# Softmax denominators of an attention block: two 128x64 products, or four 64x64 products summed afterwards

## The chip, the cores and the metric

The kernel runs on one core of one Trainium2 chip. The metric is device time in microseconds (us) of one execution. Before the change it is 3827.91 us, the median of three runs (3826.85, 3827.91, 3833.11).

The engines are named as the profile names them: PE is TensorE (its weight loads stand apart as PEld), DVE is VectorE, ACT is ScalarE, POOL is GpSimd, SP is SyncE, which here only starts transfers.

## The reference, cut to what matters

Four layers act one after the other on an image of 512 channels and 64x64 pixels, each with a group normalisation ahead of it and a residual around it. The change touches only layer 0, an attention with 8 heads of 64 channels over all 4096 pixels:

```python
def _L0_conv_ref(fmap, wq, wk, wv, wo):
    ...
    q = to_tokens(_conv1x1(fmap, wq, gain_in))
    k = to_tokens(_conv1x1(fmap, wk, gain_in))
    v = to_tokens(_conv1x1(fmap, wv, gain_in))
    AA = jnp.sum(q * q, axis=-1)
    qk = jnp.einsum('bid,bjd->bij', q, k)
    sim = -(AA[:, :, None] + AA[:, None, :] - 2.0 * qk) * scale
    attn = jax.nn.softmax(sim, axis=-1)
    out = jnp.einsum('bij,bjd->bid', attn, v)
    out = out.reshape(B, h, H, W, d).transpose(0, 1, 4, 2, 3).reshape(B, h * d, H, W)
    return _conv1x1(out, wo, gain_out)
```

The softmax needs, for every head and query, the sum of the exponentials over the 4096 keys. That sum, the denominator, is what the change computes differently. Layers 1 and 2 are gated convolutions and layer 3 is a linear attention; they follow unchanged.

## The kernel before, in words

Everything is fp32 and one product of the array leaves two records in the trace. The attention is in `_attention_pairs` and works on two heads (a pair) at a time: rows 0 to 63 of a 128-row tile are the first head, rows 64 to 127 the second. For each of the 4 pairs, `project` makes queries and keys (and, for pairs 0 and 2, the values of two pairs) with products on the whole 128x128 array. Then come 8 blocks of 512 queries. A block walks over 32 tiles of 128 keys, index `t`:

- `scores` (lines 737 to 758) makes the 128 keys x 512 queries of both heads with four products on 64x64 quarters of the array (line 745). They go into a tile `ps_s` of two PSUM banks, one bank for each head. Two exponentials on ACT (line 753), one for each head, turn it into `pt` in SBUF.
- `values` (lines 760 to 770) multiplies `pt` with the values, again by four products on 64x64 quarters (line 765). It runs two tiles behind (`AHEAD = 2`). Keys 0 to 63 accumulate in the PSUM bank `av[0]`, keys 64 to 127 in `av[1]`.
- DVE adds `pt` into `acc` (line 832), 31 additions for each block. `acc` then holds, for each of 128 key rows and each head and query, the sum over the 32 tiles.

After the last tile, ACT copies `av[0]` to SBUF as `avs` (line 837) and DVE adds `av[1]` (line 842). What remains is to sum `acc` over its 128 rows, to divide, and to check that the denominators are in a safe range. That is `close` (lines 772 to 785). It is not run at once: block `b` is closed inside block `b+1`, after the scores of `t = 3` and ahead of the values of `t = 1`. There are 28 such closes (blocks 1 to 7 of 4 pairs). Block 7 of pairs 0, 1 and 2 is closed inside the next pair's `project`, after its second product step (3 closes), and the last block between two output products at the end (1 close).

In the last pair, `output` multiplies finished blocks with the output weights, on the 128x128 array (line 792): block `b-1` after each of the blocks 1 to 6, the last two at the end.

What sets the order around the change:

- Buffers. `ps_s` has 3 tiles of two banks, taken in turn by the scores, by the `ps_d` of `close`, by the products of `project` and by `output` (through `ps_mm`, which hands out the first half of such a tile). The tile that `ps_d` takes must have been emptied by the exponentials of `t = 1`. It is next wanted by the scores of `t = 6`. `av` has two single banks. `pt` has 5 buffers. The pool `p3` has three rows of 512 under the tag `row`, for `avs`, `rd` and the `kept` tiles of `project`.
- Queues. Each engine runs its instructions in the order of its own queue. A scheduler at build time places instructions of the program text in these queues, so that DVE, for example, has an addition to `acc` between two instructions of `close`.
- `project` keeps partial sums of its products (a Strassen-like scheme of seven products, `_Seven.steps`, lines 463 to 505). Step p1 goes to a bank which ACT copies to `kept` (line 664), and step p2 may accumulate on that bank only after the copy. Line 684 is the DVE addition that ends such a sum and frees its `kept` row.

Of the kernel before, what the change touches and what calls it, by code (L numbers as in the profile page):

```python
# [10 lines left out]
FP = mybir.dt.float32  # L11
# [5 lines left out]
P = 128  # L17
# [4 lines left out]
BLK = 512  # L22
# [3 lines left out]
D = C // HEADS  # L26
# [502 lines left out]
def _attention_pairs(tc, a, X, QO, gmask, small, centered, stats, mv, okay):  # L529
# [12 lines left out]
    nc = tc.nc  # L542
# [6 lines left out]
    with tc.tile_pool(name="att1", bufs=1) as p1, tc.tile_pool(  # L549
        name="att2", bufs=2  # L550
    ) as p2, tc.tile_pool(name="att3", bufs=3) as p3, tc.tile_pool(name="pt", bufs=5) as ptp, tc.tile_pool(
        name="ps_s", bufs=3, space=PSUM
# [8 lines left out]
        ps_mm = _Halves()  # L561
# [22 lines left out]
        ones = p1.tile([P, D], FP, tag="ones", name="ones")  # L584
# [186 lines left out]

        def close(pair, b, av, acc):

            ps = ps_mm.tile([P, BLK], FP, tag="mm", name="ps_d")
            for h in range(2):
                nc.tensor.matmul(
                    ps[h * D : (h + 1) * D, :], ones, acc[:, ts(h, BLK)], start=True, stop=True
                )
            rd = p3.tile([P, BLK], FP, tag="row", name="rd")
            nc.vector.reciprocal(rd, ps)  # L780
            nc.vector.tensor_mul(QO[pair][:, ts(b, BLK)], av, rd)
            nc.vector.scalar_tensor_tensor(
                good, rd, 1.0 / SUM_HIGH, good, ALU.is_ge, ALU.mult
            )
            nc.vector.scalar_tensor_tensor(good, rd, 1.0 / SUM_LOW, good, ALU.is_le, ALU.mult)
# [17 lines left out]

        for pair in range(HEADS // 2):
            project(pair, pair and (lambda: close(*done)))
            if pair == HEADS // 2 - 1:

# [6 lines left out]
            for b in range(NB):  # L814
# [3 lines left out]
                acc = p2.tile([P, 2 * BLK], FP, tag="acc", name="acc")  # L818
                pts = {}
                for t in range(NT + AHEAD):  # L820
                    if t < NT:
                        pts[t] = scores(pair, b, t)
                    if t == AHEAD + 1 and done is not None:
                        close(*done)
                    if t >= AHEAD:
                        u = t - AHEAD
                        pt = pts.pop(u)
                        values(home(pair), av, u, pt)
                        if u == 0:
                            first = pt  # L830
                        else:
                            add = nc.vector.tensor_add(acc, acc if u > 1 else first, pt)  # L832
                            if (pair, b, u) == (HEADS // 2 - 1, *HINT_DVE):
                                past(mybir.EngineType.DVE, add)
# [11 lines left out]
            if pair == HEADS // 2 - 1:  # L846
                output(NB - 2, range(2))
                close(*done)
# [6 lines left out]
        ps = ps_mm.tile([P, BLK], FP, tag="mm", name="ps_ok")  # L855
# [1271 lines left out]
```

## Time and profile before

One execution was profiled. Its span from the first to the last instruction is 3828.3 us, beside the median of 3827.91 us without the profiler's own view.

| | busy us | share of the span |
|---|---|---|
| PE, matrix products | 3752.0 | 98% |
| PEld, weight loads | 1657.9 | 43% |
| DVE | 2688.1 | 70% |
| ACT | 2069.3 | 54% |
| POOL | 132.2 | 3% |

The granted clock of the array is 0.996 of full speed over the span. By stages, in us from the start of the span:

| from, to | what | PE busy | DVE busy | ACT busy |
|---|---|---|---|---|
| 0 to 137 | loading, normalisation, `project` of pair 0 | 105.09 | 75.41 | 41.28 |
| 137 to 587 | 8 blocks of pair 0 | 449.08 | 345.62 | 327.19 |
| 640 to 1088 | 8 blocks of pair 1 | 448.00 | 344.63 | 326.29 |
| 1190 to 1638 | 8 blocks of pair 2 | 448.00 | 344.93 | 325.72 |
| 1692 to 2252 | 8 blocks of pair 3 with the output products | 560.00 | 392.08 | 327.90 |
| 2252 to 3828.3 | layers 1 to 3 | 1532.87 | 1055.22 | 676.70 |

How to read the views. A group line names the line of the kernel, the engine, the operation, what is written and read, its shape and count, then busy us, mean ns of one, and idle time of the engine just before with what ended it. A line of the timeline has the start in us, the length in us, engine, line and operation, and in square brackets how long the engine had been idle and what released it. Up to 8 matrix instructions in a row are merged into one line with a count. Ends of matrix products are modelled, so starts are the firmer numbers.

### The profile page before, as it was taken

How to read it: one execution, taken by the hardware profiler on the slowest of the kernel's cores; microseconds unless marked ns; L12 is line 12 of the kernel's file. 1: busy time of each engine (PE TensorE's matmuls, PEld its weight loads, DVE VectorE, ACT ScalarE, POOL GpSimd, SP SyncE). 2: the span in 40 equal slices, each digit the busy share in tenths (PEclk: the TensorE clock that was granted, in tenths of full speed). 3: DMA queues.
4: the chain of work that ended last, by engine and by line, in shares of the span. 5: the costliest groups of instructions: out<-in, count | busy, mean ns of one | idle time of the engine just before them, and what ended most of it. 6: DMA issues, size and time to landing. Idle time of an engine off the chain costs nothing. (4 is left out here: it accounts for less than half of the span.)

```text
span 3828.3 us, 81625 instructions
## 1 busy us (share of the span) xinstructions
PE 3752.0 (98%) x35294; PEld 1657.9 (43%) x35294; DVE 2688.1 (70%) x3242; ACT 2069.3 (54%) x2998; POOL 132.2 (3%) x112
## 2 busy tenths in 40 slices
PE   6999999999999999999999999999999999999999
PEld 5633334333365333343333334554445544455543
DVE  6577787777765777876776757766677677665437
ACT  3577774777735777746665655663246632355210
POOL 0000000000000000000000000000000000122112
PEclk9999999999999999999999999999999999999999
DMA  2000000000000000000000015772057730564312
GB/s 100 9 1 1 1 1 9 1 1 1 1 1 9 1 1 1 1 9 1 1 1 1 1 49 168 198 201 81 13 157 194 199 102 27 151 178 103 97 56 91
DMA packets 178413, 212.91 MB, mean 56 GB/s; under 512 B 13032, under 2 KB 121832, under 8 KB 177920
## 3 DMA queue, kind: packets, MB, share of 16 engines
q1 hardware_dynamic: 151232, 148.46, 14.5%
q10 hardware_dynamic: 26784, 59.11, 4.2%
q8 instruction: 280, 4.59, 0.5%
q14 instruction: 85, 0.70, 0.1%
q0 software_dynamic: 32, 0.06, 0.0%
HBM read 147.81 MB, written 59.77 MB: 54 GB/s over the span
## 5 line engine op out<-in xcount | busy, mean ns | idle before, releaser
L753 ACT ACTIVATE pt<-ps_s,A 128x512 f32<-128x512 f32 x2048 | 1286.3, 687 | 534.8 <-PE ps_s L745 527.1
L832 DVE TENSOR_TENSOR acc<-acc,pt 128x1024 f32<-128x1024 f32 x960 | 1174.1, 1223 | 327.8 <-ACT pt L753 300.8
L745 PE MATMUL ps_s<-O,K 64*64 64x512 f32 x8192 | 1111.6, 589 | 0.0
L745 PEld LDWEIGHTS ps_s<-O,K 64*64 64x64 f32 x8192 | 334.3, 133 | 553.8 <-issue 307.1
L765 PE MATMUL av<-pt,O 64*64 64x512 f32 x4096 | 558.2, 590 | 0.9 <-ACT pt L753 0.9
L765 PE MATMUL av<-pt,V 64*64 64x512 f32 x4096 | 554.4, 590 | 0.0
L1006 ACT COPY S<-S 32x1295 f32<-32x1295 f32 (+1 forms) x272 | 341.4, 1256 | 217.4 <-DMA S<-F 105.6
L765 PEld LDWEIGHTS av<-pt,O 64*64 64x64 f32 x4096 | 171.5, 133 | 276.1 <-issue 254.9
L765 PEld LDWEIGHTS av<-pt,V 64*64 64x64 f32 x4096 | 168.3, 133 | 281.0 <-issue 270.3
L933 PE MATMUL ps<-diff,w_sum 128*128 128x512 f32 x516 | 242.0, 601 | 3.1 <-DVE w_sum L441 1.9
L933 PEld LDWEIGHTS ps_cv<-S,T 64*32 64x32 f32 x13824 | 194.1, 105 | 111.5 <-issue 73.0
L933 PE MATMUL ps_cv<-S,T 64*32 64x128 f32 x13824 | 233.6, 273 | 5.0 <-issue 2.4
L933 PE MATMUL ps<-h,w_out_L 128*128 128x512 f32 x512 | 229.6, 599 | 1.5 <-DVE X L1287 1.4
L454 DVE TENSOR_TENSOR diff<-X 128x512 f32<-128x512 f32 x200 | 134.0, 683 | 83.1 <-PE ps L933 46.4
L383 ACT ACTIVATE X<-X,gn_less 128x512 f32<-128x512 f32 x122 | 77.3, 709 | 152.0 <-DVE gn_less L125 152.0
L933 PE MATMUL ps<-X,w_in_L 128*128 128x512 f32 x304 | 145.8, 611 | 10.8 <-ACT w_in_L L391 5.4
L933 PE MATMUL ps<-h,pw_L 128*128 128x512 f32 x320 | 143.8, 599 | 1.9 <-DVE h L1275 1.6
L933 PEld LDWEIGHTS ps<-h,w_out_L 128*128 128x128 f32 x512 | 94.0, 190 | 118.3 <-issue 96.5
L933 PEld LDWEIGHTS ps<-diff,w_sum 128*128 128x128 f32 x516 | 94.6, 190 | 116.8 <-issue 106.5
L454 DVE TENSOR_TENSOR diff<-X,diff 128x512 f32<-128x512 f32 x200 | 135.3, 683 | 12.9 <-PE ps L933 11.3
L1060 DVE STREAM_TRANSPOSE h<-ps_cv 128x512 f32<-128x512 f32 x112 | 109.2, 1048 | 48.6 <-PE ps_cv L933 48.2
L933 PE MATMUL ps<-agg,w_proj 128*128 128x512 f32 x256 | 118.5, 602 | 1.0 <-DVE turned L1060 0.9
(233 smaller groups left out, 3324.7 us busy)
## 6 DMA issues: line engine op xcount, KB each, us to landing
T<-in_L_T_dram SPq DMA_DIRECT2D x112, 384.0 KB, 4.6
F<-plane ACTq DMA_DIRECT2D x112, 324.0 KB, 3.5
S<-F SPq DMA_DIRECT2D x224, 162.0 KB, 4.6
S<-G SPq DMA_DIRECT2D x96, 153.0 KB, 4.3
G<-plane ACTq DMA_DIRECT2D x48, 289.0 KB, 2.5
row<-G SPq DMA_DIRECT2D x48, 272.0 KB, 3.3
T<-in_L_T_dram SPq DMA_DIRECT2D x48, 256.0 KB, 4.1
out_dram<-y SPq DMA_DIRECT2D x32, 256.0 KB, 2.0
```

Of the source, the lines that this page charges most:

```text
L383: self.nc.scalar.activation(xs, xs, AF.Identity, bias=less)
L454: yield eng.tensor_tensor(t[j][c], a(c), b(c), ALU.subtract)
L745: nc.tensor.matmul(ps[ts(half, D), ts(h, BLK)], K[rows, t * P + half * D : t * P + (half + 1) * D], QO[pair][rows, cols], start=True, stop ...
L753: exp = nc.scalar.activation(pt[:, ts(h, BLK)], ps[:, ts(h, BLK)], AF.Exp, bias=A[:, t, h : h + 1])
L765: nc.tensor.matmul(av[half][rows, :], v[keys, t * P + h * D : t * P + (h + 1) * D], pt[keys, ts(h, BLK)], start=(t == 0), stop=(t == NT - 1),)
L832: add = nc.vector.tensor_add(acc, acc if u > 1 else first, pt)
L933: self.tc.keep_in_program_order(self.nc.tensor.matmul(*args, **kw))
L1006: nc.scalar.copy(second, first)
L1060: nc.vector.transpose(out, src)
```

## The change

Inside `close`, the ones that sum `acc` over its rows are used in two halves of 64 rows. Four products of 64x64 quarters take the place of two products of 128x64: rows 0 to 63 of `acc` go to the first bank of `ps_d`, rows 64 to 127 to the second, and within a bank the first head fills partitions 0 to 63 and the second 64 to 127. The two banks are then added: ACT copies the first to `rd`, DVE adds the second to it. The reciprocal that read PSUM before now reads and writes `rd` in SBUF. `ps_d` now has both banks of its `ps_s` tile in use, where the second stood empty before. Nothing else differs.

```diff
         def close(pair, b, av, acc):
 
-            ps = ps_mm.tile([P, BLK], FP, tag="mm", name="ps_d")
-            for h in range(2):
-                nc.tensor.matmul(
-                    ps[h * D : (h + 1) * D, :], ones, acc[:, ts(h, BLK)], start=True, stop=True
-                )
+            ps = ps_s.tile([P, 2 * BLK], FP, tag="s", name="ps_d")
+            for half in range(2):
+                keys = slice(half * D, (half + 1) * D)
+                for h in range(2):
+                    nc.tensor.matmul(
+                        ps[ts(h, D), ts(half, BLK)],
+                        ones[keys, :],
+                        acc[keys, ts(h, BLK)],
+                        start=True,
+                        stop=True,
+                    )
             rd = p3.tile([P, BLK], FP, tag="row", name="rd")
-            nc.vector.reciprocal(rd, ps)
+            nc.scalar.copy(rd, ps[:, 0:BLK])
+            nc.vector.tensor_add(rd, rd, ps[:, BLK:])
+            nc.vector.reciprocal(rd, rd)
             nc.vector.tensor_mul(QO[pair][:, ts(b, BLK)], av, rd)
             nc.vector.scalar_tensor_tensor(
                 good, rd, 1.0 / SUM_HIGH, good, ALU.is_ge, ALU.mult
```

## The prediction, made before the changed kernel had run

> **What bounds the kernel now.** I read the page's busy shares first, then busy time by stages, then the groups of `close`, and last the timelines of PE, ACT and DVE around one close (pair 0, block 2, about 254 us) and around the close inside the `project` of pair 2.
>
> ```profile
> PE 3752.0 (98%) x35294; PEld 1657.9 (43%) x35294; DVE 2688.1 (70%) x3242; ACT 2069.3 (54%) x2998; POOL 132.2 (3%) x112
> ```
>
> PE is busy for 98% of the span and in the blocks for all of it, so the array's sequence of starts sets the time there. ACT and DVE have room: about 326 and 345 of 448 us for a pair's eight blocks.
>
> A busy array can still lose time between products. The PE timeline shows where:
>
> ```profile
> 253.32 1.04 PE L745 MATMUL ps_s<-O,K 64*64 64x512 f32 x8
> 254.29 1.08 PE L776 MATMUL ps_d<-acc,ones 128*64 128x512 f32 x4
> 255.29 1.09 PE L765 MATMUL av<-pt,O 64*64 64x512 f32 x8
> 256.20 1.04 PE L745 MATMUL ps_s<-O,K 64*64 64x512 f32 x8
> 257.06 1.04 PE L765 MATMUL av<-pt,O 64*64 64x512 f32 x8
> ```
>
> Four quarters run side by side, in two passes, so scores or values of one tile take two intervals. Their length comes from weight loads far apart in a block:
>
> ```profile
> 2177.92 0.15 PEld L745 LDWEIGHTS ps_s<-O,K 64*64 64x64 f32 x4 [0.28 <-PE ps_s L745]
> 2219.12 0.15 PEld L745 LDWEIGHTS ps_s<-O,K 64*64 64x64 f32 x4 [0.28 <-PE ps_s L745]
> ```
>
> These are 24 key tiles, 96 intervals, apart: 41.20 / 96 = 0.4292 us. From the scores at 253.32 to the next at 256.20 there are six intervals (scores, `ps_d` and values, two each), or 2.575 us at that pace. It took 2.88: 0.305 us are lost around `ps_d`. From starts it splits into 0.11 ahead of `ps_d`, 0.14 ahead of the values and 0.05 after their first pass.
>
> Whole blocks say the same. The copies of `av` that end two blocks:
>
> ```profile
> 250.12 0.59 ACT L837 COPY avs<-av 128x512 f32<-128x512 f32 x1 [1.30 <-PE av L765]
> ...
> 306.23 0.59 ACT L837 COPY avs<-av 128x512 f32<-128x512 f32 x1 [1.30 <-PE av L765]
> ```
>
> A block with a close is 32 x 4 + 2 = 130 intervals, 55.79 us; it took 56.11, an excess of 0.32. Over the blocks of the first three pairs it is steadily 56.10 to 56.11. I use 0.312 for a close.
>
> **What the Trainium skill says.** "TensorEngine Tiling (Array Packing)", Tiling Modes, Key Properties: changing the tiling mode, not merely the tile, drains the engine. Scores and values use 64x64 and `ps_d` 128x64, so each close inside a block has two mode changes; the trace agrees, at 0.31 us for both. The same page, Gotcha 1 under Restrictions and Gotchas, says different row tiles cannot access one PSUM bank at the same time. This is why the four quarters need two banks and an addition; no trace tests it. "Perfetto Trace Analysis", Tensor Engine Instruction, says that ends of matrix instructions are estimated, so I count starts only; the 1.04 us lengths overlap the following starts here. "TensorE: Matmul & The Clock Gate", Architectural detail, says ACT and DVE are strict FIFO: a copy added to ACT's queue holds up the exponentials behind it if it waits.
>
> **The change part by part.** *Array.* `ps_d` becomes four quarters in two passes, two intervals of 0.4292 us, the form that line 765 already has (rows choose the bank, columns the partitions). Before, two products in two passes took two intervals too. Weight loads go from 4 to 8 records, as in every other 64x64 group, under running products. So the useful array time is unchanged and only the two mode changes go: 28 x 0.312 = 8.7 us. For the three closes in `project` and the last one the neighbours are 128x128: both mode changes stay, and I take 0 (at most the same 0.3 us each way).
>
> *Start of `ps_d`.* Without the drain it starts at 254.18. It still needs the tile that the second key tile's exponentials free. ACT runs the first four tiles' exponentials from 250.99 to 255.73, so that one is over at about 253.36, the load being wanted at about 253.75. That covers it, by 0.4 us.
>
> *ACT copy and DVE addition.* Nearest rows are the copy and addition of `avs`, of the same shapes, and the reciprocal:
>
> ```profile
> L780 DVE RECIPROCAL rd<-ps_d 128x512 f32<-128x512 f32 x32 | 107.2, 3349 | 0.0
> L842 DVE TENSOR_TENSOR avs<-avs,av 128x512 f32<-128x512 f32 x32 | 22.0, 687 | 19.3 <-ACT avs L837 18.4 <-ACT mark L840 0.9
> L837 ACT COPY avs<-av 128x512 f32<-128x512 f32 x32 | 18.8, 586 | 41.5 <-PE av L765 41.5
> ```
>
> That is 32 x 0.586 = 18.8 us more ACT and 32 x 0.687 = 22.0 us more DVE. The reciprocal from SBUF instead of PSUM is shown by no row; a tenth either way is 0.33 us for each, off the path, and I take no difference.
>
> In the queues of the changed build the copy stands behind the eight exponentials of the first four tiles, and the addition and reciprocal behind the third addition to `acc` (it was behind the second). Behind the copy waits the exponential of `t = 4`. ACT was idle there:
>
> ```profile
> 250.99 4.74 ACT L753 ACTIVATE pt<-ps_s,A 128x512 f32<-128x512 f32 x8 [0.28 <-PE ps_s L745]
> 257.31 1.26 ACT L753 ACTIVATE pt<-ps_s,A 128x512 f32<-128x512 f32 x2 [1.58 <-PE ps_s L745]
> ```
>
> The quarters are finished by about 255.3, the copy runs 255.73 to 256.32, and the scores of `t = 4`, 0.3 us earlier than now, release their exponential at about 257.0. It fits. On DVE:
>
> ```profile
> 254.78 1.23 DVE L832 TENSOR_TENSOR acc<-acc,pt 128x1024 f32<-128x1024 f32 x1
> 255.92 3.35 DVE L780 RECIPROCAL rd<-ps_d 128x512 f32<-128x512 f32 x1
> 259.19 1.16 DVE L832 TENSOR_TENSOR acc<-acc,pt 128x1024 f32<-128x1024 f32 x1
> ```
>
> The third addition takes 255.92 to 257.15, the new one ends at about 257.85 and frees `ps_d`'s tile. It is wanted by the scores of `t = 6`, whose loads would stand at about 258.9. So the release moves ahead of the need by 1 us. Today it is just late, and harmless:
>
> ```profile
> 259.32 0.15 PEld L745 LDWEIGHTS ps_s<-O,K 64*64 64x64 f32 x4 [0.39 <-DVE rd L780]
> 259.64 0.15 PEld L745 LDWEIGHTS ps_s<-O,K 64*64 64x64 f32 x4 [0.17 <-issue]
> ```
>
> The first load is 0.11 late, the second is back on the pace. This wait goes and gives nothing. The fourth addition to `acc` ends near 263.5. It gates the exponential of `t = 9` (five `pt` buffers), due near 265.6: cover 2 us.
>
> *`project`.* In pairs 1 and 3 the copy waits for a `kept` row freed by DVE at about 598.7, the addition frees the bank at about 600.6, and the addition of line 684 that p2's copy depends on moves ahead of the reciprocal: no delay. In pair 2 the order is worse:
>
> ```profile
> 1099.11 3.36 DVE L780 RECIPROCAL rd<-ps_d 128x512 f32<-128x512 f32 x1
> ...
> 1104.13 0.68 DVE L684 TENSOR_TENSOR V<-ps,kept 128x512 f32<-128x512 f32 x1
> ...
> 1103.70 0.59 ACT L664 COPY kept<-ps 128x512 f32<-128x512 f32 x1 [9.02 <-DVE O L781]
> ...
> 1104.33 0.33 PEld L458 LDWEIGHTS ps<-X,wqkv 128*128 128x128 f32 x2 [0.53 <-ACT kept L664]
> ```
>
> Today the copy starts when line 781 frees the row of `avs`, and PE's p2 starts on the pace at 1104.47. In the changed build it waits for the addition to `V` (line 684) behind the reciprocal. DVE now runs: addition to `O` until 1100.1, the new addition until 1100.75, reciprocal until 1104.1, `V` until 1104.7. So `kept` is ready at 1105.35 instead of 1104.29, and p2 starts 1.0 us late. PE is busy throughout this stage, so I count it in full: +1.0 us, once; between 0 and 2.
>
> *End.* The last quotient is finished at 2236.2 today, about 1.4 us later with the copy and addition. The output product that needs it starts after fourteen other passes, about 2240.6: hidden by 3 us.
>
> Sum: -8.7 + 1.0 = -7.7 us. The profiled span goes from 3828.3 to 3820.6. Its difference to the median is 0.4 us, so I subtract from the median: 3820.2 us.
>
> **Rivals.**
> A: no drain is saved, since the gap belongs to something else at this place (the trace credits the load of `ps_d` to an exponential). Against it: that exponential ended 0.8 us earlier, and the same long load gap stands at other changes of form. Saving 0, `project` +1: 3828.9 us.
> B: the released tile comes late. If the copy or addition gets behind one more key tile's work than I read in the queues, the tile comes free at 259.6 instead of 257.85, 0.7 us after its need. The stall repeats in 28 blocks: 28 x 0.7 = 19.6, less the saving of 8.7, plus 1: 3839.8 us. It decides from a release about 1.3 us later than mine, where the stall eats the 0.31. For it: two more links in the chain. Against it: these are the queue orders of the built program, and 1 us of slack.
> C: half of the saving stays hidden, because the wait of `ps_d` for its tile has only 0.4 us cover and a late exponential shifts it, or because `project` loses 2 to 4 us instead of 1: 28 x 0.15 = 4.2 less 1, or 8.7 less 4: about 3824 us.
>
> **How the numbers follow.** My forecast gets 0.78, A 0.06, B 0.08, C 0.08. The forecast's own range is 3818 to 3822: the excess could be 0.30 to 0.33 us, `project` 0 to 2, the four outer closes 1 us either way. About 0.2%, 7.7 us, is what a measurement of this kernel can tell from no change, and the forecast stands at that edge. One fact leans it towards the faster side: PE catches up with a late load in part (as at 259.64), and I counted the stall in `project` in full. I put 0.50 of its 0.78 beyond and 0.28 within. A and C lie within, which makes 0.42. B is slower: 0.08. The range is 3817.8 to 3826.5; it holds the forecast and C, and leaves out A and B.
>
> **What would show it.** In the PE timeline of the changed kernel, scores of `t = 3` to scores of `t = 4` take 2.58 us instead of 2.88, blocks take 55.79, `ps_d` stands as one line of 8 products 64x64, and the load that waited for `rd` waits for nothing on DVE. In `project` of pair 2 one load waits about 1 us for `kept`. I am wrong if blocks still take 56.1 (A), if the loads of line 745 wait for line 787 (the new addition) or those of `ps_d` for an exponential (B, C), or if the three `project` stages grow by more than 2 us together.

## The result, and the profile after

| | before | changed |
|---|---|---|
| median | 3831.12 us (10 runs) | 3822.26 us (10 runs) |
| span of the profiled execution | 3828.3 us | 3821.6 us (its time 3823.27 us) |
| block with a close inside, pairs 0 to 2 | 56.10 to 56.14 us, one 56.20 | 55.79 to 55.80 us |
| block of the last pair with output products | 70.19 to 70.20 us | 69.88 to 69.92 us |
| stage from pair 0 to 1, 1 to 2, 2 to 3 | 107.85, 157.86, 107.85 us | 107.89, 158.38, 107.89 us |
| first to last copy of `av` | 2029.23 us | 2020.91 us |
| from the last copy of `av` to the end | 1605.08 us | 1607.95 us |

The ratio of the times is 0.9978, with a 95% interval of 0.9969 to 0.9986: the changed kernel is faster by 8.9 us in the medians. Blocks and stages are counted from one copy of `av` to the next (line 837 before, line 845 after). The row "first to last copy of `av`" is the attention; it is 8.32 us shorter. The spans of the two profiled executions differ by less, 6.7 us: what lies ahead was 1.2 us shorter, but the layers behind the attention took 2.9 us more in that execution. The part on the scatter below comes back to this.

The busy shares of the page after:

```profile
PE 3741.6 (98%) x35422; PEld 1915.0 (50%) x35422; DVE 2717.5 (71%) x3274; ACT 2085.0 (55%) x3030; POOL 133.4 (3%) x112
```

128 more products and loads on PE (x35294 before), 32 more instructions each on DVE and ACT. PE stays the bound. Two copies of `av` that end two blocks, in the ACT timeline after:

```profile
248.53 0.59 ACT L845 COPY avs<-av 128x512 f32<-128x512 f32 x1 [1.27 <-PE av L765]
...
304.32 0.59 ACT L845 COPY avs<-av 128x512 f32<-128x512 f32 x1 [1.27 <-PE av L765]
```

They are 55.79 us apart, which is 130 intervals of 0.4292 us and nothing more. The PE timeline around `ps_d` of the same close (start, length, line, operation, count):

```profile
250.76 0.75 PE L765 MATMUL av<-pt,O 64*64 64x512 f32 x4
251.19 0.59 PE L745 MATMUL ps_s<-O,K 64*64 64x512 f32 x1
251.34 0.60 PE L765 MATMUL av<-pt,O 64*64 64x512 f32 x3
251.62 0.75 PE L745 MATMUL ps_s<-O,K 64*64 64x512 f32 x4
252.05 0.59 PE L778 MATMUL ps_d<-acc,ones 64*64 64x512 f32 x1
252.20 0.60 PE L745 MATMUL ps_s<-O,K 64*64 64x512 f32 x3
252.48 0.75 PE L778 MATMUL ps_d<-acc,ones 64*64 64x512 f32 x4
252.91 0.59 PE L765 MATMUL av<-pt,O 64*64 64x512 f32 x1
253.06 0.60 PE L778 MATMUL ps_d<-acc,ones 64*64 64x512 f32 x3
253.34 0.75 PE L765 MATMUL av<-pt,O 64*64 64x512 f32 x4
253.76 0.59 PE L745 MATMUL ps_s<-O,K 64*64 64x512 f32 x1
```

From the scores of `t = 3` (251.19) to those of `t = 4` (253.76) pass 2.57 us, where it was 2.88. The other thing to see is the counts of 1 and 3: one quarter of the array runs ahead of the other three. It starts `ps_d` at 252.05, the three follow at 252.63 (within the row at 252.48, one interval ahead of their second pass at 253.06): 0.58 us apart, and so in every row. The four quarters are four streams with a pace of 0.4292 us each. The distance arises in the first block of a pair, which has no close, in the kernel before as well; there the first `ps_d`, at the start of the second block, ends it. In the changed kernel it then stays as it is through all blocks of a pair, 0.58 us in pairs 0 and 2 and about 0.46 us in pair 1, until products in another form stand between, as the output products do in the last pair.

ACT and DVE at the same close, one timeline each:

```profile
249.43 4.74 ACT L753 ACTIVATE pt<-ps_s,A 128x512 f32<-128x512 f32 x8 [0.31 <-PE ps_s L745]
254.02 0.62 ACT L786 COPY rd<-ps_d 128x512 f32<-128x512 f32 x1
255.44 1.27 ACT L753 ACTIVATE pt<-ps_s,A 128x512 f32<-128x512 f32 x2 [0.80 <-PE ps_s L745]
```

```profile
253.22 2.56 DVE L840 TENSOR_TENSOR acc<-acc,pt 128x1024 f32<-128x1024 f32 x2
255.69 0.68 DVE L787 TENSOR_TENSOR rd<-rd,ps_d 128x512 f32<-128x512 f32 x1
256.41 3.35 DVE L788 RECIPROCAL rd<-rd 128x512 f32<-128x512 f32 x1
```

The copy follows the eight exponentials at once and is done 0.80 us before the next one can start. The addition frees the tile of `ps_d` at 256.37. The weight loads of the scores of `t = 6`, which take that tile, in the timeline of loads:

```profile
256.34 0.30 PEld L765 LDWEIGHTS av<-pt,O 64*64 64x64 f32 x4
256.77 0.13 PEld L745 LDWEIGHTS ps_s<-O,K 64*64 64x64 f32 x1
256.92 0.15 PEld L765 LDWEIGHTS av<-pt,O 64*64 64x64 f32 x3
257.20 0.30 PEld L745 LDWEIGHTS ps_s<-O,K 64*64 64x64 f32 x4
```

No load of line 745 waits for `rd` any more (before, line 780 held up such loads for 11.2 us in 28 waits). The first of the `ps_s` loads stands at 256.77, 0.40 us behind the release, that of the other three about 257.35.

### The profile page after: what moved, and what is told of

The parts are those of the page before. It is cut to its first block, busy times and chain, and to the rows that moved or that the text cites. A ratio compares the mean times of both kernels' runs of the same rounds, so it can differ in the third digit from the quotient of the medians.

```text
span 3821.6 us, 81915 instructions
## 1 busy us (share of the span) xinstructions
PE 3741.6 (98%) x35422; PEld 1915.0 (50%) x35422; DVE 2717.5 (71%) x3274; ACT 2085.0 (55%) x3030; POOL 133.4 (3%) x112
## 5 line engine op out<-in xcount | busy, mean ns | idle before, releaser
L745 PE MATMUL ps_s<-O,K 64*64 64x512 f32 x8192 | 1459.2, 589 | 0.0
L765 PE MATMUL av<-pt,O 64*64 64x512 f32 x4096 | 800.5, 589 | 0.9 <-ACT pt L753 0.9
L745 PEld LDWEIGHTS ps_s<-O,K 64*64 64x64 f32 x8192 | 483.3, 133 | 430.5 <-issue 234.8
L765 PE MATMUL av<-pt,V 64*64 64x512 f32 x4096 | 660.3, 589 | 0.0
L765 PEld LDWEIGHTS av<-pt,O 64*64 64x64 f32 x4096 | 284.2, 133 | 162.2 <-ACT pt L753 11.9
L765 PEld LDWEIGHTS av<-pt,V 64*64 64x64 f32 x4096 | 205.2, 133 | 269.0 <-issue 258.3
L941 PE MATMUL vkp<-kT,vT 128*128 128x512 f32 x256 | 115.4, 593 | 3.0 <-DVE vT L1700 2.0
```

Source lines behind the costliest of these rows:

```text
L745: nc.tensor.matmul(ps[ts(half, D), ts(h, BLK)], K[rows, t * P + half * D : t * P + (half + 1) * D], QO[pair][rows, cols], start=True, stop ...
L765: nc.tensor.matmul(av[half][rows, :], v[keys, t * P + h * D : t * P + (h + 1) * D], pt[keys, ts(h, BLK)], start=(t == 0), stop=(t == NT - 1),)
L941: self.tc.keep_in_program_order(self.nc.tensor.matmul(*args, **kw))
```

## Experiments

**Which of the two parts counts?** The form of the products and the chain behind them (copy, addition, reciprocal from SBUF) were tried apart. `form_alone` puts `ps_d` into quarters but only over rows 0 to 63, so half of each denominator is left out and one bank holds the result; the chain is that of before.

```
-  ps[h * D : (h + 1) * D, :], ones, acc[:, ts(h, BLK)], start=True, stop=True
+  ps[ts(h, D), :], ones[0:D, :], acc[0:D, ts(h, BLK)], start=True, stop=True
```

> Only the form of the products changes: two products in 64x64 quarters over rows 0 to 63 of acc, one bank, the reciprocal straight from PSUM as before. Rows 64 to 127 of acc are left out of the denominators. Theory (the drain is gone, but the tile of ps_d is now held too long: the reciprocal, which starts after the second addition to acc, frees it about 9.2 us after the block's av copy, and the scores of t = 6 now want it at about 8.3 to 8.9): blocks take 56.1 to 56.3, so nearly all of the gain is lost to the wait for rd, about 0.4 us in each block; the total is 3829 to 3833, no faster than before. Rival (as the prediction put it, that wait gives nothing and costs nothing): blocks take 55.79 and the total falls by 8 us.

`chain_alone` keeps the 128x64 products and takes the longer chain; the bank is added to its own copy, so the denominators are doubled.

```
-  nc.vector.reciprocal(rd, ps)
+  nc.scalar.copy(rd, ps)
+  nc.vector.tensor_add(rd, rd, ps)
+  nc.vector.reciprocal(rd, rd)
```

> Only the chain of ACT copy, DVE addition and reciprocal from SBUF; the products stay 128x64 and the DVE adds the same bank again, so denominators are doubled. Theory (two mode changes for each close stay): blocks take 56.10, the wait for rd is gone from the loads of line 745, the project of pair 2 is longer by 0.5 us; the total is that of before plus 0 to 1. Rival (the gain came from freeing the tile earlier, not from the form): blocks take 55.79.

`form_copy` is `form_alone` with an ACT copy that frees the bank and a reciprocal from SBUF; half of each denominator is left out here too.

> The quarters over rows 0 to 63 of acc with an ACT copy that frees the bank, and the reciprocal from SBUF; no second bank and no addition, so rows 64 to 127 are left out of the denominators. Theory (form and early release are needed together): blocks take 55.79, no load of line 745 waits for rd, total 8 to 9 us below before. Rival (two quarters behave otherwise than four, or the addition matters): blocks take more than 55.9.

| kernel | block | first to last copy of `av` | ratio to before (95%) |
|---|---|---|---|
| before, run again | 56.10 us | 2029.22 us | |
| `form_alone` | 55.84 us | 2022.10 us | 0.998 (0.9971 to 0.9989) |
| `chain_alone` | 56.10 us | 2029.60 us | 1.0002 (0.9993 to 1.0011) |
| `form_copy` | 55.79 us | 2021.80 us | 0.9978 (0.9972 to 0.9985) |

(The first close of each pair, up to 0.04 us longer in three of the four kernels, is left out of the second column, and so is one block of 56.19 us in each of the first two.) The form alone brings 0.26 of the 0.31 us of a block; the chain alone brings nothing, though it too takes away the wait of the loads for `rd`. My theory for `form_alone`, that this wait would eat most of what the form gains, fell. The loads of `form_alone` show why (in brackets the idle time before):

```profile
257.33 0.15 PEld L765 LDWEIGHTS av<-pt,O 64*64 64x64 f32 x2 [0.22 <-issue]
257.75 0.15 PEld L765 LDWEIGHTS av<-pt,O 64*64 64x64 f32 x2 [0.28 <-issue]
258.61 0.21 PEld L745 LDWEIGHTS ps_s<-O,K 64*64 64x64 f32 x8 [0.71 <-DVE rd L780]
```

The pairs of loads at 257.33 and 257.75 belong to the quarters that also did `ps_d`. Their next load was due at 258.18 and came at 258.61, 0.43 us late. But a load runs one pass, 0.43 us, ahead of its product, so the product was 0.05 us late, as the block is. (The two quarters that had no `ps_d` to do were two passes ahead and could wait.)

`form_copy` lost 0.76 us in each of the stages from pair 0 to 1 and 2 to 3 (108.61 us), where the order of PE's products around `ps_a` came out differently (that this costs the 0.76 us was not tested); the stage from pair 1 to 2 took 157.88.

**Does the loss belong to the change of form or to the place?** The denominators were summed a second time, in a block's quiet middle, in the form of each kernel (`twice_before`, `twice_after`). The copy at the end of `again` reads one element of the second sum, which is used for nothing else.

```
                         close(*done)
+                    if t == 11 and done is not None:
+                        again(done[3])
```

```
+        def again(acc):
+            ps = ps_mm.tile([P, BLK], FP, tag="mm", name="ps_e")
+            for h in range(2):
+                nc.tensor.matmul(
+                    ps[h * D : (h + 1) * D, :], ones, acc[:, ts(h, BLK)], start=True, stop=True
+                )
+            nc.scalar.copy(none, ps[0:1, 0:1])
```

In `twice_after` the four quarter products stand in `again`, in a tile of two banks from the pool of the scores.

> The kernel before, with a second set of the two denominator products in 128x64 tiles (tile `ps_e`, read only in one element) at key tile 11 of each block that has a close inside. Two more passes are 0.858 us. If the 0.31 us belong to the two changes of tiling mode, wherever they stand, these blocks go from 56.10 to 56.10 + 0.858 + 0.31 = 57.27 us. If they belong to the place behind the third scores (rival A: the wait of `ps_d` for its tile), they go to 56.10 + 0.858 = 56.96.

> The changed kernel, with a second set of the four quarter products (tile `ps_e`, read only in one element) at key tile 11 of each block that has a close inside. If no change of mode means no loss, blocks go from 55.79 to 55.79 + 0.858 = 56.65 us. If four more quarters bring a loss of their own at a place where nothing waits, 56.8 or more.

Measured, in one execution each: blocks of 57.27 us in `twice_before` and 56.65 us in `twice_after`, both to 0.01 us what the theory of the mode changes gives. The PE timeline of `twice_before` at the new place:

```profile
267.15 1.04 PE L765 MATMUL av<-pt,O 64*64 64x512 f32 x8
268.01 1.04 PE L745 MATMUL ps_s<-O,K 64*64 64x512 f32 x8
268.98 1.08 PE L791 MATMUL ps_e<-acc,ones 128*64 128x512 f32 x4
269.99 1.09 PE L765 MATMUL av<-pt,O 64*64 64x512 f32 x8
270.90 1.04 PE L745 MATMUL ps_s<-O,K 64*64 64x512 f32 x8
```

Groups are 0.86 us apart (267.15 to 268.01); into the 128x64 form it takes 0.97, out of it 1.01, and 0.91 behind: 0.11 + 0.15 + 0.05 = 0.31 us, the split seen at the first place. The 0.31 us are the price of going from 64x64 to 128x64 tiles and back. Rival A fell.

It is not that the 128x64 products themselves are slow. The second pass of `ps_e` starts 0.48 us after the first, and so does that of the 64x64 values behind it: 0.05 us over the pace in both. Each of the two changes costs about 0.16 us, 0.11 or 0.10 up to the first start and 0.05 up to the second. The loads show how. In the timeline of loads of `twice_before`:

```profile
268.01 0.15 PEld L745 LDWEIGHTS ps_s<-O,K 64*64 64x64 f32 x4 [0.28 <-issue]
268.98 0.20 PEld L791 LDWEIGHTS ps_e<-acc,ones 128*64 128x64 f32 x4 [0.81 <-ACT pt L753]
269.99 0.21 PEld L765 LDWEIGHTS av<-pt,O 64*64 64x64 f32 x8 [0.81 <-issue]
```

Within the stream a load stands a pass ahead of its product. At each change of form it starts together with its product instead (268.98 and 269.99 in both timelines), which agrees with a drain. In `twice_after` the first load of `ps_e` keeps its lead of 0.43 us:

```profile
267.32 0.13 PEld L801 LDWEIGHTS ps_e<-acc,ones 64*64 64x64 f32 x1
```

```profile
267.75 0.59 PE L801 MATMUL ps_e<-acc,ones 64*64 64x512 f32 x1
```

**How late may the tile come free?** One (`late1`) or three (`late3`) operations on `rd` that leave it as it is, ahead of the new addition:

```
+            for _ in range(3):
+                nc.vector.scalar_tensor_tensor(rd, rd, 1.0, rd, ALU.mult, ALU.max)
             nc.vector.tensor_add(rd, rd, ps[:, BLK:])
```

> The changed kernel with one more operation of 0.68 us on `rd` ahead of the new addition, which leaves `rd` as it was: the tile of `ps_d` comes free at 257.07 instead of 256.37. The loads of the scores of t = 6 stand at 256.77 (one quarter) and 257.35 (three) and run a pass ahead of their products, so nothing is lost: blocks of 55.79 to 55.85 us, the total within 2 us of the changed kernel. Rival: PE has no slack at the release, then each block gains up to 0.68 us and the total 19 us.

> As late1 with three such operations: the tile comes free at 258.4. The three quarters that load at 257.35 are 1.1 us late, of which the 0.43 us by which a load runs ahead of its product hides a part: blocks of 56.5 us (56.3 to 57.1), the total +20 us (+14 to +37) on the changed kernel, and the loads of line 745 wait for `rd`. If the place of the release doesn't matter at all, blocks of 55.79 us and no change.

In one execution each, `late1` has blocks of 55.79 us (span 3819.3 us), `late3` of 56.83 us, with three longer ones (span 3855.6 us, time 3857.3 us: slower than the kernel before, 3832.05 us in the same series). DVE and loads of `late1`:

```profile
256.69 0.69 DVE L789 TENSOR_TENSOR rd<-rd,ps_d 128x512 f32<-128x512 f32 x1
```

```profile
257.13 0.14 PEld L765 LDWEIGHTS av<-pt,O 64*64 64x64 f32 x3 [0.28 <-issue]
257.49 0.21 PEld L745 LDWEIGHTS ps_s<-O,K 64*64 64x64 f32 x5 [0.21 <-issue]
```

The release at 257.38 makes the first quarter's load, due at 257.12, 0.37 us late, and it costs nothing. DVE, loads and PE of `late3`:

```profile
258.96 0.69 DVE L789 TENSOR_TENSOR rd<-rd,ps_d 128x512 f32<-128x512 f32 x1
```

```profile
257.92 0.18 PEld L765 LDWEIGHTS av<-pt,O 64*64 64x64 f32 x4 [0.25 <-issue]
259.77 0.24 PEld L745 LDWEIGHTS ps_s<-O,K 64*64 64x64 f32 x8 [1.66 <-ACT pt L753]
```

```profile
257.92 1.07 PE L765 MATMUL av<-pt,O 64*64 64x512 f32 x8
259.80 1.09 PE L745 MATMUL ps_s<-O,K 64*64 64x512 f32 x8 [0.81 <-DVE rd L789]
```

The loads were due at 258.35 and came at 259.77, just behind the release at 259.65 (the view of loads names an exponential, long done; PE's names `rd`). 1.42 us late, less the pass by which they run ahead, makes 1.0, and the block is 1.04 us longer. I had taken the three operations at 0.68 us each; with the gaps they moved the addition by 2.22 us (258.96 against 255.69, each counted from its own copy of `av`, 249.58 and 248.53), and the stall came out above the 0.7 us of the expectation, within its range. `late1` moved it by 0.79 us for nothing. If each microsecond beyond the free ones costs one in a block, 2.22 - 1.04 = 1.2 us are free; this is an estimate, as no run lies between the two. `late3` is rival B made real.

**Is there a better mixture?** `hybrid` takes the new form only inside blocks and leaves the three closes in `project` and the last one as they were.

```
-                        close(*done)
+                        close(*done, inside=True)
```

(`close` picks the old or the new body by `inside`.)

> Quarters, copy and addition only in the closes that stand inside a block; the closes in `project` and the last one keep the form of before. Blocks of 55.79 us as in the changed kernel; the stage from pair 1 to pair 2 goes from 158.38 back to 157.86, if the +0.5 us there come from the longer chain (copy, addition, reciprocal) ahead of the addition to `V`. If they come from anything else in the changed kernel, they stay. The total is 0.5 us below the changed kernel, which the times can't tell from nothing: ratio to before 0.997 to 0.999.

> The changed kernel again. Blocks of 55.79 us and 2020.9 us from the first to the last copy of `av`, as before; the rest of the span (1608 us behind the last copy) moves by 2 or 3 us, if what it lost there against the kernel before is scatter between executions. The ratio to before 0.9970 to 0.9985.

The attention went as expected: blocks of 55.79 us, the stage from pair 1 to 2 at 157.90 us, 2020.41 us in all against 2020.90. But the median was 3825.83 us (ratio 0.9987, 0.9981 to 0.9994) beside 3823.31 us for the changed kernel in the same series (0.9979, 0.9971 to 0.9987). Both went again:

> The kernel of `hybrid` again, beside the changed kernel, since its median stood 2.5 us above that of the changed kernel while its attention was 0.5 us shorter. If that was scatter between executions, the two medians come within 1.5 us of each other, in either order, and the time behind the last copy of `av` goes with the granted clock. If the mixed form costs something behind the attention, it stands 2 to 3 us above again.

> The changed kernel for comparison: 2020.9 us from the first to the last copy of `av`, ratio to before 0.997 to 0.9985.

3827.84 us (0.9987, 0.998 to 0.9995) beside 3824.86 us (0.998, 0.9972 to 0.9989). The mixture stands 2.5 and 3.0 us above again, so by the expectation on record this isn't scatter alone, though the intervals overlap. Its attention is shorter in both traces, and behind the last close the order of instructions on PE, ACT, DVE, POOL and SP is the same in both kernels. What makes it longer there stays open. One part can be seen, in the busy times of a 200 us stretch in the layers behind the attention; the number before the DMA share is the granted clock. `hybrid` and `hybrid_2`:

```profile
2414.20:2614.20 200.00, 193.61 (x3566) 100.04 (x3565) 142.24 (x205) 121.51 (x107) 0.00 (x0) 0.98 0.64 177
```

```profile
2414.20:2614.20 200.00, 194.95 (x3667) 101.55 (x3666) 142.61 (x206) 123.19 (x107) 0.00 (x0) 1.00 0.64 177
```

The same program got a clock of 0.98 in one execution and 1.00 in the other; behind the last copy of `av` they took 1613.7 and 1609.7 us. Counted at the same products, these 4.0 us are lost inside this stretch, so the clock can account for the distance between the two executions of `hybrid` (0.02 of 200 us), but not for two medians above those of the changed kernel. No version was found that beats the changed kernel.

## The prediction, step by step

**Array: right.** 28 x 0.312 = 8.7 us was the saving. Added up, the 28 blocks are 8.92 us shorter. Most gained 0.31 us; I had overlooked that the first close of each pair stands in a block of 56.13 to 56.14 us before, where the quarters also come together again, and that one block took 56.20. That the loss goes with the changes of mode, of which the Trainium skill, "TensorEngine Tiling (Array Packing)", Tiling Modes, Key Properties, says that they drain the engine, is shown by the second set of products: another 0.31 us at another place in the 128x64 form, none in quarters.

**"This wait goes and gives nothing": right, nearly.** `chain_alone` removes it and gains nothing in a block; `form_alone` keeps it, 0.43 us late at its load, and loses 0.05 us.

**Start of `ps_d`, copy and addition: right.** Counted from its copy of `av`, this close stands 1.59 us earlier than before (248.53 against 250.12). The copy was put at 255.73, so here at 254.14, and ran at 254.02. Its cost was taken from the copy of `avs`, 586 ns; the rows of the tile `ps_d` after show (shortest, median and longest, ns):

```profile
L786 ACT COPY rd<-ps_d x32: 586/625/629, 198.2 to 2221.7; 128x512 f32<-128x512 f32 x32
L787 DVE TENSOR_TENSOR rd<-rd,ps_d x32: 677/681/689, 199.9 to 2222.4; 128x512 f32<-128x512 f32 x32
```

It is 625 ns in 28 of 32 cases, where it follows exponentials at once; the 0.04 us more lie in ACT's idle 0.80 us. The reciprocal from SBUF takes 3352 ns, from PSUM 3349: no difference, as I took it.

One sign that I had named for rival C is there, at no cost: a load of `ps_d` that comes just behind an exponential. The quarter that runs ahead has used up the cover of 0.4 us. In the timeline of loads after, its first load follows the end of the second tile's exponentials (about 251.86) and stands 0.14 us ahead of its product at 252.05, where 0.43 is usual; the product is still on the pace, 0.43 us after the one before (251.62).

```profile
251.91 0.44 PEld L778 LDWEIGHTS ps_d<-acc,ones 64*64 64x64 f32 x5
```

**Release of the tile: right.** I had 257.85, so 256.26 here; it was 256.37. The slack of 1 us came out as 1.2 (`late3`). It is made up otherwise than I thought: the quarter that runs ahead has its load only 0.40 us behind the release, the others 1.0, and the load's own lead of one pass is added to that. Rival B was to decide from a release 1.3 us later than mine, where the stall eats the 0.31 us; by the estimate from `late3` it is 1.2 + 0.31 = 1.5 us. The chain used none of it.

**`project` of pair 2: the wait right, its price wrong.** This is the term of the sum that was mis-sized: +1.0 us in the prediction, +0.52 in the stage, of which only 0.17 at the wait that I had worked out. That the total came within half of mine is luck. The longer chain causes 0.47 of it: `chain_alone` has 158.33 us there without any quarter, `hybrid` 157.90 with quarters in the blocks alone. The wait itself came as worked out. DVE, ACT and loads there, after:

```profile
1095.18 3.35 DVE L788 RECIPROCAL rd<-rd 128x512 f32<-128x512 f32 x1
1098.45 0.63 DVE L684 TENSOR_TENSOR V<-ps,kept 128x512 f32<-128x512 f32 x1
```

```profile
1099.16 1.18 ACT L664 COPY kept<-ps 128x512 f32<-128x512 f32 x2 [5.06 <-DVE V L684]
```

```profile
1099.80 0.30 PEld L458 LDWEIGHTS ps<-X,wqkv 128*128 128x128 f32 x2 [0.73 <-ACT kept L664]
```

This part stands 5.59 us earlier than before (DVE's addition of line 494 at 1092.07 against 1097.66). So `kept` is ready at 1099.75 + 5.59 = 1105.34; I had 1105.35. The load follows, 1.06 us behind the one before (1104.33). But I compared two starts and overlooked what PE does meanwhile: it now runs six products of `diff,w_sum` ahead of this load where it ran four, so the load is only 0.73 - 0.24 = 0.49 us behind its pace, and by its lead the product still less. From the first products of `X,wqkv` to those of `X,w_sum` PE takes 8.76 us after (1095.44 to 1104.20) and 8.59 before (1101.03 to 1109.62): 0.17 us are lost at the wait. Of the rest, 0.05 us are lost on the way in and 0.29 where the next block's first exponentials start (5.42 us ahead of before until the last item of `project`, 5.13 from there). ACT there, before and after:

```profile
1191.29 4.74 ACT L753 ACTIVATE pt<-ps_s,A 128x512 f32<-128x512 f32 x8 [2.54 <-DVE A L728]
```

```profile
1186.16 4.74 ACT L753 ACTIVATE pt<-ps_s,A 128x512 f32<-128x512 f32 x8 [2.83 <-PE ps_s L745]
```

Before, the first exponential starts 0.09 us after `A` is ready (1191.20). After, it starts 0.39 us after `A` (1185.77), just as the scores of the second tile are done (1186.15). All three traces of the changed kernel show this, and so do `chain_alone`, `late1` and `late3`; the traces without the new addition in this stage do not. The prediction had no such term. The two losses come apart: `twice_after` has the wait for `kept` but not this one, and its stage takes 158.08 us; `late1`, where DVE makes the addition to `V` ahead of the reciprocal, has this one but no loss at `kept`, and takes 158.20. Why the built program waits there for the second tile stays open.

**The other two stages and the end: right in what they cost.** 107.89 for 107.85 us, twice. The last quotient is finished 0.95 us later than before, counted from the last copy of `av` (1.4 in the prediction), and the output products behind `ps_d` run through without a gap in both kernels.

**The sum.** -8.92 + 0.60 = -8.32 us in the attention, against -7.7 in the prediction; its two larger errors, in the array and in `project`, go the same way. The 3820.2 us were counted from a median of three runs, 3827.91. From that of ten, 3831.12, they would have been 3823.4; the measured 3822.26 lies between the two.

**What was to be seen, and was not.** `ps_d` does not stand as one line of eight products: the skew splits it into 1, 4 and 3. In `late3`, where the stall brings the quarters together, it is one line of eight, and the pace is the same.

**Scatter.** The three comparisons of medians give -8.9, -7.9 and -7.3 us for the changed kernel, each with an interval of some 3 us either way; the attention, -8.3 in every trace, fits them. In the profiled executions the part behind the last copy of `av` took 1605.1 and 1604.2 us for the kernel before (I had expected a distance of 1 to 5 us between these two; it was 0.9), 1608.0, 1608.5 and 1609.4 for the changed one, and 1605.6 for `late1`, which has the changed kernel's form. So some 3 us of a difference between two spans can come from layers whose instructions have the same order in both. The second trace of the kernel before was a quick execution, 3828.23 us where the median of its series is 3832.80. Adding to each such part the distance of its execution from the median gives an estimate of 1608.8 us for the kernel before and 1608.9 for `chain_alone`, and of 1606.9, 1608.3 and 1609.5 for the changed kernel, 1606.5 for `form_alone` and 1607.4 for `form_copy`. This shows no share of the changed form; for `hybrid` it gives 1609.9 and 1612.7.

## What to carry to other kernels

On an array that is never idle, compare the time of a block with the number of passes times the pace: the excess is what products lose between them, and a change of tile form in the middle of a stream is one such loss (0.31 us there and back, at both places tried). Removing it is worth the extra operations on other engines only while these end ahead of the next need of the buffer they hold; here 0.8 us of delay were free (by estimate 1.2), and 2.2 us turned a gain of 9 us into a loss of 25. And when a wait is predicted, ask what the waiting engine has been given to do ahead of it in the new order, and by how much its loads run ahead: 1.06 us between two starts were 0.17 us on the path.

## What the runs showed of the hardware that was not expected

- In 64x64 quarters the streams need not run together: from the first block of a pair on one quarter ran 0.58 us (in pair 1 0.46) ahead of the three others, with products of `ps_s`, `ps_d` and `av` running side by side, at no cost in pace. In these traces `ps_d` in 128x64, or a stall of all four (`late3`), brought them together.
- Where the form changes between 64x64 and 128x64, a load starts together with its product instead of one pass ahead, and each change costs about 0.16 us (`twice_before`).
- A load that comes up to 0.43 us late (`form_alone`), or 0.37 (`late1`), costs 0.05 us or nothing, since it runs one pass ahead of its product; 1.42 us late costs 1.04.
- The copy of a 128x512 PSUM tile on ACT took 625 ns right behind exponentials and 586 ns elsewhere.
- One program was granted a clock of 0.98 and of 1.00 in the same 200 us stretch of two executions.
